# A small copy on GpSimd between the first product of weights and values and the table's transfers

## The chip, the cores and the metric

The kernel runs on one core of a Trainium2 chip. The metric is the device time of one execution in microseconds (us). Before the change the median of three runs is 1701.59 us (1696.14 to 1702.38).

The engines are named as the profile names them: PE is TensorE (PEld its weight loads), DVE is VectorE, ACT is ScalarE, POOL is GpSimd, SP is SyncE, which here only issues transfers. Each engine takes its instructions in order and waits for semaphores of the others.

## The reference

Four layers follow each other on x of 2 batches x 2048 tokens x 256, each added to x: a state-space layer, a mixture of experts, an attention layer and the same mixture of experts again. The change is in the attention layer and in what it shares its time with, the routing of the second mixture.

```python
x = x + attn_a(layernorm(x))            # state space
x = x + ffn(layernorm(x))               # experts, 2 of 8 for each token
x = x + attn_b(layernorm(x))            # attention, below
x = x + ffn(layernorm(x))               # experts, same weights
```

The attention mixes over the first axis of its input, which is the batch, and there are only 2 entries: for each token and each of 16 heads a softmax over two scores. The output is then a weighted sum of two value vectors, projected by w_out and added.

```python
q, k, v = jnp.split(qkv, 3, axis=-1)
scores = jnp.einsum('ibnd,jbnd->ijbn', q, k) * scale
attn = jax.nn.softmax(scores, axis=1)
attn_out = jnp.einsum('ijbn,jbnd->ibnd', attn, v)
return x + attn_out.reshape(slen, bsz, NUM_HEAD * HEAD_DIM) @ w_out.T
```

In an expert layer a router takes the two best of eight experts for each token, and each token's result is the weighted sum of two small networks.

## The kernel before

All products are in float32. Tokens are handled in groups of 512 (four tiles of 128); a group is (b, s), batch b of 2 and stretch s of 4. The attention handles both batches of a stretch together, since it mixes over them; so its loop runs over s = 0 to 3.

**Attention.** A softmax over two scores is a sigmoid of their difference. So the kernel works with xd, the difference of the two normed inputs.
- `scores(s, ts)` (L1328): for each tile of 128 tokens and each half of the heads PE makes pk (keys of xd, PSUM bank A) and two pq (queries of each batch, banks B and C); ACT scales pk into kd (L1351), DVE multiplies (qk, L1355) and sums over the head (L1356).
- `weights(s)` (L1365): ACT's sigmoid, a transpose on PE, a copy to SBUF (prow, L1375), a store to DRAM (prob, L1376), and eight loads on SP (L1382) that repeat each row of prob over 64 partitions: o[0] and o[1], one for each batch, each in four pieces, first those of the value blocks c = 0 to 3, then of 4 to 7. Each of the eight is 512 KB on the SBUF side. Then pv (L1392) adds one batch's own value part.
- `mix(s)` (L1405): for each c of 8 PE makes pvd, the values of xd (L1410, bank A), and DVE multiplies it into o[0] and o[1] in place (L1418).
- `outward(s)` (L1423): for each batch and each pair of tiles PE projects o with w_o (pao, L1430, bank C) and DVE adds to x (L1438). After each batch the routing of its group, `prepared`, is put in line.

Every PSUM bank name (A, B, C, T) has two buffers; PE can be two products ahead of the engine that reads them.

The order of a turn of the loop (L1457): the first half of scores(s + 1), mix(s), outward(s), the second half of scores(s + 1), weights(s + 1). The pieces of other work are generators in `aside`; each call of `aside.step` takes some steps of them: `front` (loads and layer norm of a later stretch), `prepared` and `entered`.

**Routing of the second expert layer.** For each group `prepare` (L309) stores x to the output and the normed xn to DRAM. Its layer norm (L234) has one small step on POOL: rs_g (L244), the power -0.5 of the variance, between DVE's statistics (L239, L240, L243) and DVE's xn_g (L248). PE transposes xn_g (pt_g, L257) and makes the router's scores (pr_g, L330); DVE ranks them and works out a slot in a table in DRAM for every token (L345 to L410). `enter` (L413) then writes the table by indirect transfers from POOL: once, ahead of all others, 16 transfers of `rest` (L420), which fill free slots; then for every group 8 transfers of `pay` (L433). The L433 wait for all L420. Each of these moves 128 rows of 12 bytes. After groups 4 and 6 `plan_early` picks tiles of experts that are already full; SP loads their table rows (tab_ge, L656) and weights (w_ge, L668 and L670), POOL gathers their tokens (xs_ge, L683), PE works on them within the attention stage (L722, L752), and POOL scatters the results (L776).

**What sets the order.** A scheduler orders the traced instructions of each engine but SP, whose order is that of the program. `pool(i)` notes the last instruction of POOL given to it, and the table's transfers are traced in a block that puts them behind that instruction on POOL:

```python
on_pool = []
def pool(i):
    on_pool[:] = [i.ins]
...
with tc.issue_after(on_pool[0]):
    i = nc.gpsimd.indirect_dma_start(out=self.table, ...)
```

Before the change the instruction noted last, where the table's transfers of the attention stage are traced, is a step of a layer norm: rs_l (L1289) or rs_g (L244).

`entered` for the two groups of stretch s is put in line just ahead of mix(s + 1), and mix takes its steps after every second c.

Of the kernel before, what the change touches and what calls it, by code (L numbers as in the profile page):

```python
# [8 lines left out]
F32 = mybir.dt.float32  # L9
# [4 lines left out]
P = 128  # L14
# [32 lines left out]
def kernel(  # L47
# [24 lines left out]
    nc = tc.nc  # L72
# [7 lines left out]
    lnp = ctx.enter_context(tc.tile_pool(name="ln", bufs=2))  # L80
    ps = ctx.enter_context(tc.tile_pool(name="ps", bufs=2, space=bass.MemoryType.PSUM))

    def bank(tag, name):
        return ps.tile([P, 512], F32, tag=tag, name=name)
# [145 lines left out]
    def pool(i):  # L230
        on_pool[:] = [i.ins]
# [994 lines left out]
    with tc.tile_pool(name="att1", bufs=1) as a1, tc.tile_pool(name="att2", bufs=2) as a2:  # L1226
# [178 lines left out]
        def mix(s):  # L1405
            xd, o = inputs.pop(s)[1], mixing[s]
            for c in range(NA):
                pvd = bank("A", f"pvd_{s}{c}")
                for k in range(KD):
                    nc.tensor.matmul(  # L1410
                        pvd,
                        w_qkv_sb[:, k, 2, c * P : (c + 1) * P],
                        xd[:, k, :],
                        start=(k == 0),
                        stop=(k == KD - 1),
                    )
                for i in range(2):
                    nc.vector.tensor_tensor(o[i][:, c, :], pvd, o[i][:, c, :], ALU.mult)  # L1418
                if c % 2:
                    aside.step(2)  # L1420
            mixed.add(s)
# [35 lines left out]
        for s in range(NS):  # L1457

            if s + 1 < NS:
                while s + 1 not in inputs:  # L1460
                    aside.step()
                scores(s + 1, range(0, GT // 2))

                aside.waiting.insert(0, entered())
            else:
                aside.rest()
                tiles.step(4)
            mix(s)
            outward(s)
            if s + 1 < NS:  # L1470
                scores(s + 1, range(GT // 2, GT))
                weights(s + 1)
# [68 lines left out]
```

## Time and profile before

| | |
|---|---|
| median of three runs | 1701.59 us (1696.14 to 1702.38) |
| the profiled execution | 1703.7 us, of which the span from its first to its last instruction is 1702.0 |
| mean granted TensorE clock | 0.97 |
| busy: PE, DVE, ACT, POOL | 1585.8, 896.3, 674.6, 739.0 us |
| PE busy in 0 to 700 us, 700 to 940, 940 to 1400, 1400 to 1702 | 627.7, 227.6, 440.7, 289.8 us |
| transfers by SP's queue, by POOL's queue | 193.42 MB, 36.42 MB |

The four stretches of the third last row are, about: the state-space layer with part of the first expert layer, the rest of that layer, the attention, the rest of the second expert layer.

Lines of the timelines give start, length, engine, line of the kernel, operation, output<-inputs, shapes, the number of merged instructions, and in brackets the idle time before the first of them and what ended it. Buffer numbers are left out of names: o is o[0] or o[1] of any stretch. A transfer's line on POOL or SP is its issue; how long the data took is in the DMA view, "us to landing". "q0 software_dynamic" there is the queue of POOL's transfers, "q1" that of SP's.

### The profile page before, as it was taken

Reading aid. Unit: us, or ns where it says so; the run is one execution under the profiler, and the core shown is the slowest. Engines: PE = TensorE matmul, PEld = TensorE weight load, DVE = VectorE, ACT = ScalarE, POOL = GpSimd, SP = SyncE. Lnnn points to the kernel's source line nnn. Section 1 sums busy time; section 2 is a strip of 40 time slices with the busy share of each in tenths; the row PEclk is TensorE's granted clock in tenths of the full one; section 3 lists DMA queues with packets and bytes.
Section 4 is the critical chain, followed back from the end, with each engine's and each line's share of the span. In section 5 each row is a group of like instructions: output and inputs, shape, how many; then the busy total and the mean of one; then the engine's idle time right before and its main releaser. Section 6 shows DMA issues by size and latency. Waiting matters only on the chain.

```text
span 1702.0 us, 22149 instructions
## 1 busy us (share of the span) xinstructions
PE 1585.8 (93%) x7088; PEld 1194.0 (70%) x7088; DVE 896.3 (53%) x2471; ACT 674.6 (40%) x1340; POOL 739.0 (43%) x702
## 2 busy tenths in 40 slices
PE   6997988989999989999998999899999979999997
PEld 3665555677767767788984575465768768888886
DVE  6778878837648464422227648447454512222222
ACT  5886867856647543222332202011120322333332
POOL 3356457455545556634441003414140751544443
PEclk9998988999989999999999999999999989999999
DMA  4122211743525455889852312516353686888783
GB/s 157 39 63 49 87 47 41 215 125 89 157 48 176 104 148 134 204 261 315 233 112 78 82 43 62 89 50 138 106 107 104 184 226 179 224 236 225 229 215 51
DMA packets 174744, 231.30 MB, mean 136 GB/s; under 512 B 45920, under 2 KB 138080, under 8 KB 174368
## 3 DMA queue, kind: packets, MB, share of 16 engines
q1 hardware_dynamic: 143520, 193.42, 38.7%
q0 software_dynamic: 31104, 36.42, 11.9%
q8 instruction: 58, 0.95, 0.2%
q14 instruction: 62, 0.51, 0.1%
HBM read 192.72 MB, written 37.06 MB: 135 GB/s over the span
## 4 chain that ended last, share of the span: by engine, by line
PE 46%; DMA 7%; DVE 1%; issue 1%; POOL 1%; SPq 0%; ACT 0%; DVEq 0%; POOLq 0%
PE pab_g L722 9%; PE pao L1430 7%; PE pq L1336 6%; PE pab_f L722 5%; PE pf_g L752 4%; PE pvd L1410 3%; PE pab_ge L722 3%; PE pk L1336 3%; DMA out_dram<-y_g,tab_g 2%; PE pf_f L752 2%; DMA o<-prob 2%; PE pf_ge L752 1%; PE pr_g L330 1%; DMA xs_f<-xnd_f,tab_f 1%; DMA resid<-y_f,tab_f 1%
## 5 line engine op out<-in xcount | busy, mean ns | idle before, releaser
L722 PE MATMUL pab_g<-xT_g,w_g 128*128 128x256 f32 (+1 forms) x896 | 181.4, 361 | 0.0
L722 PE MATMUL pab_fe<-xT_fe,w_fe 128*128 128x256 f32 x672 | 158.3, 390 | 20.7 <-DVE gT_fe L731 17.8
L722 PEld LDWEIGHTS pab_g<-xT_g,w_g 128*128 128x128 f32 x896 | 158.4, 190 | 19.6 <-ACT xT_g L713 0.4
L722 PEld LDWEIGHTS pab_fe<-xT_fe,w_fe 128*128 128x128 f32 x672 | 128.8, 195 | 47.7 <-DVE gT_fe L731 22.3
L776 POOL DMA_INDIRECT out_dram<-y_g,tab_g x51 | 80.3, 1575 | 137.0 <-DVE y_g L765 54.9
L730 ACT ACTIVATE sa_g<-pab_g,b_g 128x256 f32<-128x256 f32 (+1 forms) x112 | 51.0, 455 | 188.0 <-PE pab_g L722 188.0
L731 DVE SCALAR_TENSOR_TENSOR gT_g<-pab_g,b_g,sa_g 128x256 f32<-128x256 f32 (+1 forms) x112 | 51.5, 460 | 128.9 <-ACT sa_g L730 128.9
L1336 PE MATMUL pq<-w_qkv_sb,axT 128*128 128x512 f32 x256 | 117.4, 597 | 0.0
L1006 DVE SCALAR_TENSOR_TENSOR xc<-pre,conv_w_sb,xc 128x512 f32<-128x512 f32 x144 | 113.5, 798 | 5.2 <-ACT xc L998 4.6
L1430 PE MATMUL pao<-w_o_sb,o 128*128 128x256 f32 x512 | 112.3, 380 | 0.0
L1430 PEld LDWEIGHTS pao<-w_o_sb,o 128*128 128x128 f32 x512 | 97.0, 190 | 15.9 <-issue 2.9
L989 PE MATMUL pc<-xT,w_in_sb 128*128 128x512 f32 x192 | 96.3, 631 | 0.4 <-ACT xc L998 0.4
L722 PE MATMUL pab_f<-xT_f,w_f 128*128 128x256 f32 (+1 forms) x512 | 96.4, 346 | 0.0
L433 POOL DMA_INDIRECT table_g<-pay_g,at_g x64 | 62.3, 974 | 71.2 <-DVE w_g L409 39.2
L752 PE MATMUL pf_g<-w_g,gT_g 128*128 128x256 f32 x408 | 92.7, 379 | 0.0
L722 PEld LDWEIGHTS pab_f<-xT_f,w_f 128*128 128x128 f32 x512 | 85.5, 191 | 9.4
L1043 ACT ACTIVATE lt<-lb,cum 128x128 f32<-128x128 f32 x256 | 82.8, 394 | 19.8 <-DMA lb<-sums 19.8
L1336 PEld LDWEIGHTS pq<-w_qkv_sb,axT 128*128 128x128 f32 x256 | 48.4, 191 | 57.9 <-issue 56.2
L776 POOL DMA_INDIRECT resid<-y_fe,tab_fe x42 | 67.0, 1595 | 38.2 <-DVE y_fe L765 22.6
L731 DVE SCALAR_TENSOR_TENSOR gT_fe<-pab_fe,b_fe,sa_fe 128x256 f32<-128x256 f32 x84 | 39.7, 480 | 81.3 <-ACT sa_fe L730 81.2
L1351 ACT ACTIVATE kd<-pk 128x512 f32<-128x512 f32 x32 | 19.1, 597 | 159.1 <-PE pk L1336 90.7
L752 PEld LDWEIGHTS pf_g<-w_g,gT_g 128*128 128x128 f32 x408 | 75.4, 190 | 9.3 <-DVE gT_g L731 0.2
(477 smaller groups left out, 3381.9 us busy)
## 6 DMA issues: line engine op xcount, KB each, us to landing
w_g<-in_wl_dram SPq DMA_DIRECT2D x28, 1024.0 KB, 7.5
w_fe<-in_wl_dram SPq DMA_DIRECT2D x21, 1024.0 KB
lb<-sums SPq DMA_DIRECT2D x32, 512.0 KB, 5.8
w_f<-in_wl_dram SPq DMA_DIRECT2D x16, 1024.0 KB, 6.5
o<-prob SPq DMA_DIRECT2D x32, 512.0 KB, 15.6
w_g<-in_wl_dram SPq DMA_DIRECT2D x28, 512.0 KB, 4.0
w_fe<-in_wl_dram SPq DMA_DIRECT2D x21, 512.0 KB, 6.7
w_ge<-in_wl_dram SPq DMA_DIRECT2D x9, 1024.0 KB, 8.4
```

The lines of the kernel that those rows point to most:

```text
L433: i = nc.gpsimd.indirect_dma_start(out=self.table, out_offset=bass.IndirectOffsetOnAxis(ap=at[:, t, c : c + 1], axis=0), in_=pay[:, t, c, ...
L722: nc.tensor.matmul(p[:, q * n : (q + 1) * n], t["w1"][:, k, c * P : (c + 1) * P], t["xT"][:, k, :], start=(k == 0), stop=(k == KD - 1),)
L730: nc.scalar.activation(sa[:, :n], p[:, 0:n], AF.Silu, bias=t["b1"][:, i : i + 1])
L731: nc.vector.scalar_tensor_tensor(t["gT"][:, i, :n], p[:, n : 2 * n], t["b1"][:, NHT + i : NHT + i + 1], sa[:, :n], ALU.add, ALU.mult)
L752: nc.tensor.matmul(pos[h][:, h * DM : (h + 1) * DM], t["gT"][:, j, h * P : (h + 1) * P], t["w2"][:, j, :], start=(j == 0), stop=(j == NHT ...
L776: j = nc.gpsimd.indirect_dma_start(out=self.acc if self.direct else self.acc[: self.seq[i][4] or NT + TT, :], out_offset=bass.IndirectOffs ...
L989: nc.tensor.matmul(pc, w_in_sb[:, k, DI + c * P : DI + (c + 1) * P], xT[:, k, :], start=(k == 0), stop=(k == KD - 1),)
L1006: nc.vector.scalar_tensor_tensor(xc[:, c, :], pre[:, c, j : j + TG], conv_w_sb[:, c, j : j + 1], xc[:, c, :], ALU.mult, ALU.add,)
L1043: nc.scalar.activation(lt[:, i, :], lb[:, i, :], AF.Relu, bias=g["cum"][:, t, i : i + 1], scale=-1.0)
L1336: nc.tensor.matmul(p, src[:, k, t * P : (t + 1) * P], w_qkv_sb[:, k, j, half * TG : (half + 1) * TG], start=(k == 0), stop=(k == KD - 1),)
L1410: nc.tensor.matmul(pvd, w_qkv_sb[:, k, 2, c * P : (c + 1) * P], xd[:, k, :], start=(k == 0), stop=(k == KD - 1),)
L1430: nc.tensor.matmul(po[:, j * DM : (j + 1) * DM], o[i][:, c, (t + j) * P : (t + j + 1) * P], w_o_sb[:, c, :], start=(c == 0), stop=(c == NA ...
```

## The change

In `mix`, after the products of the first value block, POOL copies one column of o[1] into a tile of its own, which nothing reads; `pool` notes the copy. There are four such copies in the kernel, one for each stretch.

```diff
                 for i in range(2):
                     nc.vector.tensor_tensor(o[i][:, c, :], pvd, o[i][:, c, :], ALU.mult)
+                if c == 0:
+
+                    come = lnp.tile([P, 1], F32, tag="come", name=f"come{s}")
+                    pool(nc.gpsimd.tensor_copy(come, o[1][:, c, 0:1]))
                 if c % 2:
                     aside.step(2)
```

In the order that the scheduler makes of it, the instructions of PE, DVE, ACT and SP stand as before. On POOL the copy of s = 0 stands ahead of the first rs_g; that of s = 1 ahead of the 16 transfers of L420 and the 16 of L433 that follow them; that of s = 2 ahead of the next 16 of L433; that of s = 3 behind the 16 transfers of L433 of stretch 2 and some gathers and scatters, ahead of the next rs_g. After the copy of s = 1 POOL's order is: 16 of L420, 16 of L433, rs_g twice, the copy of s = 2, 16 of L433, four gathers (L683), rs_g twice.

## The prediction

> **What bounds the kernel now.** I read the page first: TensorE (PE) is busy 93% of the span and holds 46% of the chain that ended last, so a change of order elsewhere counts only where PE waits. The diff touches the attention stage (about 940 to 1400 us), so next came the chain and the timelines of that stage.
>
> The chain of waits around the second mix (s = 1), columns start, length, what:
>
> ```profile
> 1059.41 0.91 PE pt_m L257 x8
> ...
> 1060.42 23.41 DMA o<-prob
> ...
> 1083.85 0.70 DVE o L1418
> ```
>
> The timeline of PE over the same mix:
>
> ```profile
> 1074.74 3.60 PE L1410 MATMUL pvd<-axd,w_qkv_sb 128*128 128x512 f32 x8
> 1084.60 12.04 PE L1410 MATMUL pvd<-axd,w_qkv_sb 128*128 128x512 f32 x24 [6.26 <-DVE o L1418]
> 1096.47 27.79 PE L1430 MATMUL pao<-w_o_sb,o 128*128 128x256 f32 x128
> 1124.10 1.88 PE L1336 MATMUL pk<-w_qkv_sb,axd 128*128 128x512 f32 x4
> 1125.81 3.60 PE L1336 MATMUL pq<-w_qkv_sb,axT 128*128 128x512 f32 x8
> ```
>
> PE starts the mix at 1074.74, fills both buffers of bank A, and sits until DVE can multiply o[1], which waits for a transfer of probabilities issued at 1060.42. The first mix has no such hole: its 32 matmuls take 13.80 us (980.39 to 994.19 in the chain). Here 1074.74 to 1096.47 is 21.73. **The hole is worth 21.73 - 13.80 = 7.9 us.**
>
> Why is that transfer slow? The DMA view of the first mix's transfers (955 to 1000 us), then of the second's (1050 to 1090); the GB/s row has 40 equal slices:
>
> ```profile
> GB/s 0 0 0 0 42 16 25 275 206 226 200 226 204 211 211 206 220 204 218 195 228 200 226 193 67 9 0 0 0 0 0 0 0 0 0 0 0 0 0 0
> ...
> o<-prob SPq DMA_DIRECT2D x8, 512.0 KB, 8.6
> ```
>
> ```profile
> GB/s 0 0 0 2 2 67 1 1 2 28 39 0 219 193 39 55 90 80 137 253 181 158 172 97 27 23 33 181 268 184 100 160 182 244 207 229 229 187 143 55
> ...
> q0 software_dynamic: 512, 0.03, 1.4%
> ...
> o<-prob SPq DMA_DIRECT2D x8, 512.0 KB, 23.4
> table_g<-rest_g,free POOLq DMA_INDIRECT x16, 13.4
> ```
>
> Alone, the 4 MB run at a flat 200 GB/s or so. Beside the table's transfers they fall below 60 several times. Those transfers start where GpSimd (POOL) is free, right after the last rs_l; POOL's timeline:
>
> ```profile
> 1049.69 1.63 POOL L1289 TENSOR_TENSOR rs_l<-rs_l,mhalf 128x8 f32<-128x8 f32 x1 [5.30 <-DVE rs_l L1288]
> 1051.49 1.06 POOL L420 DMA_INDIRECT table_g<-rest_g,free  x1 [0.17 <-issue]
> ...
> 1068.12 0.96 POOL L420 DMA_INDIRECT table_g<-rest_g,free  x1 [0.31 <-issue]
> 1077.66 0.96 POOL L420 DMA_INDIRECT table_g<-rest_g,free  x1 [8.58 <-DMA table_g<-rest_g,free]
> ...
> 1090.00 0.96 POOL L433 DMA_INDIRECT table_g<-pay_g,at_g  x1 [10.12 <-DMA table_g<-rest_g,free]
> ...
> 1109.80 0.95 POOL L433 DMA_INDIRECT table_g<-pay_g,at_g  x1 [0.30 <-issue]
> 1112.53 1.04 POOL L244 TENSOR_TENSOR rs_g<-rs_g,mhalf 128x4 f32<-128x4 f32 x1 [1.78 <-DVE rs_g L243]
> ```
>
> The last two lines matter most: the 32 transfers end at 1110.75, and rs_g, which DVE asks for at 1112.4, stands behind them on POOL with 1.78 us to spare.
>
> **The change, part by part.** In the changed program the order on PE, DVE, ACT and SP is what it was; POOL's differs by four copies alone. Copies 0 and 3 stand in POOL's idle time (69.39 us before 1010.02, 28.15 us before 1298.76) and hold up nothing: 0. Copy 1 stands ahead of the 32 transfers of s = 1, copy 2 ahead of 16 of s = 2, and each waits for o[1]'s first product of its mix. No copy of 128x1 is in the trace; the nearest are a copy of 128x18 at 0.20 us (L985) and another at 0.85 (L1016), and a memset of 128x1 at 0.10. It is an added instruction, so no gain; I take 0.2, ends 0.1 and 0.85.
>
> *Gain in mix 1.* With the transfers held back, o[0] is multiplied at 1076.80 as before and o[1] directly after, done at 1076.80 + 1.29 = 1078.09. That needs its transfer landed by 1077.5, 17 us after the issue at 1060.42. In s = 3, beside weight loads, the same product could start 16.2 us after the first of its issues (1253.98 to 1270.20); in s = 0 all eight were through 22 us after theirs, and the first four go first. PE then runs through: -7.9 us. Ends: -6.3 (only the hole itself) and -7.9.
>
> Here a rule of the Trainium skill speaks against the gain. DMA: Bandwidth & Descriptors, section SWDGE vs HWDGE vs iDMA, has the software queue and SP's queue in separate internal queues of each DMA engine, served in turn by packets. By that the table's packets should delay the others only by their own time, 1.4% of the 40 us window or 0.6 us, and holding them back would gain 0.6. This trace doesn't agree: 23.4 us to landing against 8.6 for the same transfers of s = 0. By the rule the sum below would be +6 and not -0.3. I take the rows, and keep the rule's case as a rival, since s = 2 kept some 210 GB/s beside 16 table transfers (landing 17.4).
>
> *Cost at rs_g of s = 1.* The transfers now start late, and rs_g is still behind them. POOL wakes 0.15 after DVE (1112.38 to 1112.53), copy 0.2, next start 0.17: first L420 at 1078.6. Sixteen at 1.28 start to start (16.63 / 13): the last at 1097.8. L433 waits for it to land: 3.0 to 4.4 for the four issued before o<-prob, 5.8 for the median L433 after 1090, 6.9 the longest; I take 4.4, then 0.8 from landing to start (1078.92 + 10.3 to 1090.00): 1103.0. Sixteen L433 take 20.75 (1090.00 to 1110.75): 1123.8. So POOL is taken for 45.2 us against 59.3 before, but 27 us later. rs_g starts at 1124.1, DVE's xn_g 1.08 later (1112.53 to 1113.61), its four take 1.38, and the queued x<-pao 0.69: done at 1127.2.
>
> Behind that wait on DVE stand x<-pao of the second batch, its statistics and all qk of the next scores; they free the buffers of bank C. PE goes on through both remaining pao, pk and the first pq, and stops at the second pq, which needs the C buffer that x<-pao frees. Before, that pq began at 1125.81 + 1.72 = 1127.53, thus 1119.6 with 7.9 taken off. **PE waits 1127.2 - 1119.6 = 7.6 us.** By the ends of landing: 6.2 (3.0), 9.0 (5.8), 10.1 (6.9); the copy adds up to 0.65. The next stop, the fifth pq, needs the buffer that qk's first product frees: DVE is done with it near 1133.7, PE gets there near 1135.8, so no second hole.
>
> *Cost in s = 2.* No gain: PE went into that mix at 1175.58 without a wait. The 16 L433 move from 1152.71 to 1178.92 + 0.5 = 1179.4, the last is issued at 1199.2 and lands near 1205 (5.8). Behind it on SP are the first two tab_ge (8 us behind the last L433 before), the weights of two tiles, three more tab_ge and the stores of s = 2: all some 20 us later, and first used by PE at 1247.4: hidden. On POOL four gathers wait for tab_ge, 2.75 after its issue: 1207.8 to 1212.5, and rs_g moves from 1205.44 to 1212.8. DVE's xn_g is done at 1215.3, and PE's pt_g that reads it stood at 1217.00: **hidden by 1.7 us**; past that, each us costs one.
>
> *Sum.* -7.9 + 7.6 + 0 = -0.3 us. On the profiled 1703.7 (span 1702.0 and 1.7 outside it) that is 1703.4. That run was 2.1 above the median 1701.59, so I predict 1701.3.
>
> **Rivals.**
> 1. *The table is not what slows o<-prob* (the rule above, and s = 2). Copy 1 then ends near 1084.9 and the same 45.2 us end at 1130; x<-pao at 1133.7 against pq at 1127.5: +6, or 1707.6. Against it: s = 0 has no table transfer and no dip.
> 2. *Slower: the block on POOL stays long.* If the moved transfers land as slowly as before (POOL taken for 59.3 us), rs_g starts 14.1 later still and PE waits 21.7: 7.9 is won, +13.8 in all, 1715.4. It passes 0.5% (8.5 us) where the block exceeds 45.2 + 8.8 = 54 us. For it: waits of 8.58 and 10.12 stand in the trace. Against: both fell beside o<-prob, which is over by about 1080.
> 3. *The gain without the price:* -7.9, 1693.7. The block would have to end by 1116.2, 37.6 us after its start, while 31 steps of 1.28 alone are 39.7. Only a partial form is left, with the smallest landing: -1.7.
> 4. *The bind does nothing,* because the transfers are not moved: the program's order on POOL excludes it.
>
> **How the numbers follow.** The sum with its ends (1699 to 1706): 0.58. Rival 1 (1706 to 1709): 0.14. Rival 2 (1709 to 1716), with a hole in s = 2 as its small form: 0.20. Rival 3 and gains I do not see (1692 to 1698): 0.08. The range 1695 to 1712 leaves out the far half of rivals 2 and 3. About 0.5% (8.5 us) is what a measurement of this kernel can tell from no change: faster by more 0.06, within 0.76, slower by more 0.18.
>
> **What would show it.** PE's pvd of s = 1 in one piece of about 14 us with no wait for DVE's o; o<-prob landing in 9 to 13 us with a flat GB/s row; the first L420 about 3 us after PE's second mix starts; DVE's xn_g waiting near 21 us for POOL's rs_g once (1104.5 to 1125.1), where its longest wait is 1.5 now; PE waiting 6 to 9 us at a pq after the second pao. I am wrong if xn_g does not wait (then faster), or if L420 or L433 wait for landings of over 8 us again (then slower), or if pt_g of s = 2 waits for xn_g.

## The result, and the profile after

The changed kernel takes 1704.2 us (median of 22 runs, 1697.5 to 1710.9) against 1697.8 of before on the same chip (22 runs, 1686.7 to 1707.1): a ratio of 1.0029, 95% interval 1.0015 to 1.0043, or 4.9 us slower (1697.8 x 0.0029). I had forecast 0.3 us faster: the sign and the sum were wrong.

The second mix went as forecast. I call the 16 transfers of L420 the fill, the 16 of L433 the token transfers, and all that the copy of s = 1 now holds back on POOL, up to rs_g, the block. The timeline of PE after (columns: start, length, engine, line, operation, tiles, shapes, count, idle time before and what ended it; lines from L1422 on stand four higher than before):

```profile
1070.69 13.96 PE L1410 MATMUL pvd<-axd,w_qkv_sb 128*128 128x512 f32 x32
1084.49 27.79 PE L1434 MATMUL pao<-w_o_sb,o 128*128 128x256 f32 x128
1112.11 1.88 PE L1336 MATMUL pk<-w_qkv_sb,axd 128*128 128x512 f32 x4
1113.83 1.88 PE L1336 MATMUL pq<-w_qkv_sb,axT 128*128 128x512 f32 x4
1128.40 3.78 PE L1336 MATMUL pq<-w_qkv_sb,axT 128*128 128x512 f32 x4 [12.69 <-DVE x L1442]
1131.97 3.07 PE L1336 MATMUL pk<-w_qkv_sb,axd 128*128 128x512 f32 x4
```

From pvd to pao it is 13.80 us where before took 21.73: the hole of 7.9 is gone. The DMA view of 1050 to 1090 us shows why: from 1054 to 1072 us, while o<-prob runs, the rate is flat, and the first table transfer is issued at 1074.44.

```profile
GB/s 0 66 0 109 276 199 229 197 215 211 197 229 197 219 211 197 229 199 219 211 193 233 195 31 0 0 2 2 18 1 1 2 2 2 1 1 2 0 1 2
```

But at the second pq PE waits 12.69 us and not the forecast 7.6, and the four pq behind the hole take 3.78 us instead of 1.88, the next four pk 3.07. The timeline of POOL after has the reason for the first of these:

```profile
1074.09 0.19 POOL L1422 COPY come<-o 128x1 f32<-128x1 f32 x1 [26.82 <-DVE o L1418]
1074.44 1.08 POOL L420 DMA_INDIRECT table_g<-rest_g,free  x1 [0.16 <-issue]
...
1094.02 0.95 POOL L420 DMA_INDIRECT table_g<-rest_g,free  x1 [0.30 <-issue]
1104.86 0.96 POOL L433 DMA_INDIRECT table_g<-pay_g,at_g  x1 [9.89 <-DMA table_g<-rest_g,free]
...
1124.31 0.95 POOL L433 DMA_INDIRECT table_g<-pay_g,at_g  x1 [0.30 <-issue]
1125.28 1.05 POOL L244 TENSOR_TENSOR rs_g<-rs_g,mhalf 128x4 f32<-128x4 f32 x1
```

The copy costs 0.19. Between the last fill (L420) and the first token transfer (L433) POOL waits 9.89 us for the landing, with o<-prob long over. The block from 1074.44 to 1125.28 is 50.8 us where I had 45.2, and rs_g starts as soon as it ends. The waits of the attention stage (engine, tile, line, releaser: sum, count, longest):

```profile
DVE xn_g L248 <- POOL rs_g L244: 37.7, 8, 26.0
...
PE pq L1336 <- DVE x L1442: 12.7, 1, 12.7
```

The second reason is PE's clock. A table by stretches has the granted clock behind the five engines' busy times (1.00 is full), then the DMA share and GB/s. After:

```profile
1070.70:1084.50 13.80, 13.80 (x34) 5.94 (x33) 10.83 (x16) 0.00 (x0) 8.01 (x9) 1.00 0.21 39
1084.50:1112.00 27.50, 27.50 (x129) 24.22 (x128) 5.98 (x15) 0.00 (x0) 13.25 (x14) 1.00 0.08 21
1112.00:1140.00 28.00, 15.31 (x30) 6.42 (x29) 10.60 (x25) 1.20 (x2) 12.27 (x13) 0.76 0.17 57
...
1128.40:1132.00 3.60, 3.60 (x5) 1.53 (x6) 2.66 (x10) 0.00 (x0) 0.72 (x1) 0.50 0.72 257
...
1134.90:1140.00 5.10, 5.10 (x13) 2.27 (x12) 3.36 (x4) 0.60 (x1) 0.00 (x0) 1.00 0.24 85
```

The clock is at half when PE comes back, and full again from 1134.90 on. The same table of before gives 0.84 for its mix with the hole (0.56 for 1084.60 to 1088.00, right behind it), and 1.00 after it. So the new hole costs 12.7 and 3.1 more ((3.78 - 1.88) + (3.07 - 1.88)), and the measure that I use from here on, the start of the second mix to the start of the third, goes from 100.8 us (1074.74 to 1175.58) to 108.8 (1070.69 to 1179.50): -7.9 and +15.9.

This pair of profiles shows +8.0 where the medians show 4.9 (2.5 to 7.3). Nothing in step s = 2 took the difference back: from the third mix to the fourth it is 72.8 us in both. The two executions can't be compared as wholes: after's ended 4.3 us earlier (1697.7 against 1702.0), because its first mix began 4.1 us earlier and all that follows the last pao took 378.6 us against 388.8 (from the fourth mix to the last pao it was 2.0 longer). The same changed kernel took 393.2 there in e10 below, so this is no gain of the change that I could claim.

In s = 2 the change was hidden, as forecast: the copy starts at 1182.91, rs_g at 1212.93, and PE waits for nothing at pt_g.

### The profile page after: what moved, and what is told of

The parts are those of the page before. It is cut to its first block, busy times and chain, and to the rows that moved or that the text cites. A ratio compares the mean times of both kernels' runs of the same rounds, so it can differ in the third digit from the quotient of the medians.

```text
span 1697.7 us, 22159 instructions
## 1 busy us (share of the span) xinstructions
PE 1583.7 (93%) x7088; PEld 1192.0 (70%) x7088; DVE 894.6 (53%) x2471; ACT 674.7 (40%) x1340; POOL 737.0 (43%) x706
## 4 chain that ended last, share of the span: by engine, by line
PE 47%; DMA 5%; POOL 3%; DVE 1%; issue 1%; ACT 0%; SPq 0%; DVEq 0%; POOLq 0%
PE pab_g L722 9%; PE pq L1336 6%; PE pab_f L722 5%; PE pao L1434 5%; PE pf_g L752 4%; PE pk L1336 3%; PE pab_ge L722 3%; PE pf_f L752 3%; PE pvd L1410 2%; DMA out_dram<-y_g,tab_g 2%; PE pf_ge L752 1%; POOL table_g L433 1%; POOL table_g L420 1%; PE pr_g L330 1%; DMA xs_f<-xnd_f,tab_f 1%
## 5 line engine op out<-in xcount | busy, mean ns | idle before, releaser
L1336 PE MATMUL pq<-w_qkv_sb,axT 128*128 128x512 f32 x256 | 120.3, 609 | 12.7 <-DVE x L1442 12.7
L1434 PEld LDWEIGHTS pao<-w_o_sb,o 128*128 128x128 f32 x512 | 97.0, 190 | 15.9 <-issue 2.9
L752 PE MATMUL pf_fe<-w_fe,gT_fe 128*128 128x256 f32 x336 | 79.3, 389 | 2.2 <-DVE gT_fe L731 2.2
```

What stands on the lines that cost most here:

```text
L752: nc.tensor.matmul(pos[h][:, h * DM : (h + 1) * DM], t["gT"][:, j, h * P : (h + 1) * P], t["w2"][:, j, :], start=(j == 0), stop=(j == NHT ...
L1336: nc.tensor.matmul(p, src[:, k, t * P : (t + 1) * P], w_qkv_sb[:, k, j, half * TG : (half + 1) * TG], start=(k == 0), stop=(k == KD - 1),)
L1434: nc.tensor.matmul(po[:, j * DM : (j + 1) * DM], o[i][:, c, (t + j) * P : (t + j + 1) * P], w_o_sb[:, c, :], start=(c == 0), stop=(c == NA ...
```

## The experiments

My theory: the copy of s = 1 (copy 1) closes the hole in the mix and pays for it at rs_g, with a price set by the length of POOL's block: issues, landing, issues. Rivals: copy 2 (of s = 2) carries the loss; or any table transfer, not only this order, does harm wherever it lies. Twelve runs follow; "stretch" is the start of the second mix to that of the third, from PE's timeline. All but e8 are timed beside before on the same chip, where before has medians of 1721 to 1725 us.

| run | what is different | stretch, us | ratio to before | 95% interval |
|---|---|---|---|---|
| before (first chip) | | 100.8 | | |
| after (first chip) | four copies | 108.8 | 1.0029 | 1.0015 to 1.0043 |
| e1 | copy of s = 1 alone | 107.3 | 1.0033 | 1.0018 to 1.0048 |
| e2 | copy of s = 2 alone | 103.7 | 1.0011 | 0.9996 to 1.0026 |
| e3 | L433 of two groups behind rs_g | 102.1 | 1.0004 | 0.9988 to 1.0021 |
| e4 | before, no fill | 100.3 | 0.9985 | 0.9967 to 1.0002 |
| e5 | after, no fill | 92.9 | 0.9946 | 0.9925 to 0.9967 |
| e6 | after, fill to another table | 112.7 | 1.0069 | 1.0046 to 1.0092 |
| e7 | fill and L433 behind rs_g | 119.4 | 1.0106 | 1.0077 to 1.0136 |
| e8 | e3 once more | 103.1 | a single run | |
| e9 | e3, paced | 102.2 | 0.9994 | 0.9983 to 1.0006 |
| e10 | after itself | 106.8 | 1.0008 | 0.9993 to 1.0023 |
| e11 | e9, four buffers of at_g | 92.9 | 0.9940 | 0.9919 to 0.9960 |
| e12 | e3, four buffers of at_g | 101.7 | 0.9994 | 0.9978 to 1.0010 |

The stretch accounts for the times: with e2, whose second mix has before's order, as the base (103.7 us), a difference of the stretches over 1723 us gives e5 and e11 -0.63%, e6 +0.52%, e7 +0.91%, e1 +0.21%, e10 +0.18%, all within the measured intervals. Before was not profiled on these chips; with its 100.8 of the first chip as the base, e10 (+0.35%) falls outside.

**Which copy.** e1 keeps the copy of s = 1 alone, e2 that of s = 2 alone:

```diff
-                if c == 0:
+                if c == 0 and s == 1:
```

> Only the copy of s = 1 is kept. Theory (all of the price is the block of 32 table transfers that copy 1 moves ahead of rs_g of s = 1): as the whole change, about +5 us or 1.003; PE's second mix in one piece of 13.8, then a wait of PE near 12.7 us at the second pq behind x<-pao, DVE's xn_g waiting 26 us for rs_g once. Rival (the price comes from copy 2, which makes table rows, weights and gathers of the early tiles later): copy 1 alone is at 0 to -3 us, and PE's stretch from the third to the fourth mix is shorter than with the whole change.

> Only the copy of s = 2 is kept. Theory: nothing, 1.000 within 0.2%: the hole in the second mix stays at about 6.3 us (o<-prob landing near 23), the gathers and rs_g of s = 2 come 4 to 8 us later than before and no PE instruction waits for them. Rival (price in s = 2 or in the early tiles): +2 to +5 us, with PE waiting at pt_g of s = 2 or longer from the start of mix 3 to its end (37.2 before, 39.2 with the whole change).

Measured: e1 slower by 0.33%, with the mix in one piece and PE's wait of 11.2 us at the pq; e2 keeps the hole (6.0 us) and shows no clear difference. Copy 1 carries gain and price; for copy 2 neither shows.

**The price apart from the gain.** e3 leaves the fill behind the copy and puts the token transfers of both groups behind the two rs_g of s = 1; the order on the other four engines stays:

```diff
-                aside.waiting.insert(0, entered())
+                aside.waiting.insert(0, filled() if s == 1 else entered())
...
+            if s == 1:
+                aside.add(token_rows())
```

> All four copies kept; of the 32 transfers behind copy 1 the 16 of L433 are traced later, behind both rs_g of s = 1; the order on PE, DVE, ACT and SP is that of the change. Theory: the gain stays (mix 2 in 13.8 us) and the price goes, since 16 fill transfers end 20.5 us after the copy, ahead of DVE's request for rs_g: -7 to -8 us against before, 0.995 to 0.996; DVE's xn_g waits at most 2 us for rs_g, PE has no wait at the pq after the second pao. Rival (the price is the copies, or the table being later at all): +3 to +8 us against before, since here the table's rows of the first groups come later still.

Measured: no clear difference (1.0004), not the theory's 0.995. The mix is whole and PE doesn't wait at the pq, so the price at rs_g is gone; but DVE and ACT wait at sc_g and kd, and then PE. DVE's line, and PE's, of e3:

```profile
1151.01 0.19 DVE L338 TENSOR_TENSOR sc_g<-pr_g,br_sb 128x32 f32<-128x32 f32 x1 [8.77 <-remote]
```

```profile
1153.95 0.60 PE L363 MATMUL pk_g<-sel_g,tri 128*128 128x32 f32 x2 [6.30 <-DVE sel_g L357]
```

"Remote" means that the profile finds no work that ended when the signal came. PE's pr_g are over at 1144.12, so DVE got their signal 6.9 us late; by the records of signals, three of PE's came together at 1150.99 to 1151.09, just behind the last of 16 token transfers (issued 1147.34). So a new wait took the place of the old one. It comes back below; first the other side, the gain.

**Does the fill alone slow o<-prob?** e4 is before without the 16 transfers of L420; the filling of free slots is left out.

> The kernel before without the 16 fill transfers (L420): free slots of the table keep their first contents, so that part of the computation is left out. The 16 of L433 then start right behind rs_l, at the place of the fill. Theory (it is the fill transfers that slow o<-prob, at about 2 us each to land, where L433 beside o<-prob in s = 2 left its rate alone): the hole in the second mix goes, -7 to -8 us, 0.995. Rival (any table transfer beside o<-prob slows it): the hole stays at 4 us or more, -1 to -4 us.

Measured: 0.9985, no clear difference; the rival's case. The token transfers then start beside o<-prob, and the mix still has two small holes (1.93 and 2.22 us). Its DMA view from 1060 to 1105 us dips to 51 even without the fill:

```profile
GB/s 0 0 0 0 1 0 58 3 1 1 1 1 40 18 44 15 25 36 261 254 206 214 216 194 70 51 73 130 236 228 204 224 217 229 208 186 124 53 0 0
```

So both kinds of table transfer can cost beside o<-prob. The rule weighed in the prediction (the Trainium skill, DMA: Bandwidth & Descriptors, section SWDGE vs HWDGE vs iDMA: queues served in turn, so 0.6 us by the prediction's estimate) does not hold for these rows, since holding the transfers back gave 7.9. It is not refuted everywhere: in s = 2 of before, 16 token transfers run beside the same eight loads and the rate stays flat (1150 to 1184 us):

```profile
GB/s 0 0 0 0 0 79 2 19 2 2 32 7 116 195 227 261 212 195 228 224 198 221 212 214 210 224 200 216 210 216 211 195 197 238 180 102 25 0 0 0
```

What makes the difference between s = 1 and s = 2 was not tried.

**The block's length.** e5 is after without L420 (the filling is left out): a block of 16 issues and no landing to wait for.

> The changed kernel without the 16 transfers that fill the free slots (L420); the filling is left out, so that the copy is followed on GpSimd by the 16 token transfers alone. My theory (the price is the length of GpSimd's block between the copy and rs_g: 16 issues of 1.28 us, 10.1 us of landing, 16 issues more): the block falls from 50.8 to about 21 us, rs_g no longer waits for it (it is wanted about 28 us after the copy), PE has no hole at the pq after the second mix, its clock doesn't drop there, and the second mix stays in one piece (13.4 us): 7.9 us less than before, a ratio of 0.995. Rival (the price comes from the copy's wait itself or from the binding, whatever is behind it): still 10 us or more of waiting at that pq, a ratio near 1.003.

Measured: 0.9946, as the theory has it. POOL of e5:

```profile
1088.75 0.19 POOL L1413 COPY come<-o 128x1 f32<-128x1 f32 x1 [26.82 <-DVE o L1409]
1089.10 1.08 POOL L424 DMA_INDIRECT table_g<-pay_g,at_g  x1 [0.16 <-issue]
...
1108.68 0.96 POOL L424 DMA_INDIRECT table_g<-pay_g,at_g  x1 [0.30 <-issue]
1115.21 1.04 POOL L244 TENSOR_TENSOR rs_g<-rs_g,mhalf 128x4 f32<-128x4 f32 x1 [5.57 <-DVE rs_g L243]
```

rs_g now waits for its own input and not for POOL. The copy, the order behind it and the move to a later time are the same as in after; only the block is 20.5 us long and not 50.8. The rival that the copy's wait, or binding transfers to it, costs as such is out.

e6 was to take the landing alone out of the block: the fill goes to a table that nobody reads (the free slots are not filled), and L433 waits for nothing.

```diff
-                                out=self.table,
+                                out=self.aside,
...
-                        self.freed.append(i.ins)
```

> The changed kernel with the 16 fill transfers written to a table of their own that nobody reads (so the free slots are not filled), and the token transfers without their wait for them: 32 issues and no landing between. Theory: the block is 50.8 less 9.1 of waiting, 41.7 us; PE's hole at the pq falls from 12.7 to about 3.6 us; if the clock is not halved after so short a hole the sum is 7.9 less 3.6, 4.3 us less than before, a ratio of 0.9975; if it is, about 0.999. Rival (the landing is not the term that was mis-sized, the issues behind it are slowed as much): the hole stays near 12 us, a ratio of 1.003.

Both expectations failed: 1.0069. The issues did close up to 41 us (1098.17 to 1138.91), but PE itself slowed down in the middle of it. PE of e6:

```profile
1108.22 14.50 PE L1434 MATMUL pao<-w_o_sb,o 128*128 128x256 f32 x66
...
1127.06 0.58 PE L1434 MATMUL pao<-w_o_sb,o 128*128 128x256 f32 x1 [1.02 <-issue]
1129.16 1.28 PE L1434 MATMUL pao<-w_o_sb,o 128*128 128x256 f32 x2 [1.52 <-issue]
1132.66 0.58 PE L1434 MATMUL pao<-w_o_sb,o 128*128 128x256 f32 x1 [2.22 <-issue]
...
1142.46 13.35 PE L1434 MATMUL pao<-w_o_sb,o 128*128 128x256 f32 x51 [0.82 <-issue]
```

and DVE's second x<-pao waited 22.27 us, "remote" too, some 21 us past the end of its matmuls. From 1122.7 to 1142.4 PE did 6.0 us of work, waiting for nothing that the profile names, and was at full work again 3.5 us after the last of the 32 (1138.91). It may be that the pause of 9 us for the landing, which I wanted out of the block, had kept the transfers from piling up; no run shows that. Because of PE's stall, e6 says nothing on the size of the landing term.

**A better place for the block?** e7 puts all 32 behind the two rs_g. Its edit, against e3:

```diff
-            yield from last.fill()
-            for _ in range(8):
+            for _ in range(16):
                 yield
```

> The fill and the token transfers of the second and third group both behind the two rs_g of the second step, everything else in the order of the changed kernel on every engine. Theory: the second mix in one piece (7.9 us less than before), no price at rs_g, and a block of GpSimd of 51 us from about 15 us before the third product chain, over before the copy of the third step: a ratio of 0.995. Rival (as in the run that moved only the token transfers: a signal of PE reaches VectorE and ScalarE some 6 us late near the end of a series of transfers, wherever it lies, and PE waits for it): a ratio of 1.000.

> The kernel of e3_split once more, for its trace alone. If the 8.8 us that VectorE and ScalarE waited at sc_g and kd there belong to this order of the work, they come again at the same place; if they are an accident of that execution, the stretch from the end of the second mix to the third is near 79.5 us instead of 88.8.

Measured: e7 1.0106, the slowest of all; the rival's late signal is there (sc_g waits 8.5 us), and a second wait, which I hadn't foreseen. e8 shows e3's stall again at the same place (8.62 us), so it belongs to this order and not to one execution. The new wait of e7:

```profile
1171.70 0.16 DVE L391 TENSOR_TENSOR at_g<-lo_g,hi_g 128x4 int32<-128x4 f32 x1 [14.44 <-DMA table_g<-pay_g,at_g]
```

The row numbers at_g have two buffers, and a token transfer reads them from SBUF: moved late, it holds up the group after next, and PE stands 13.49 us behind that.

**Pace, and buffers.** e9 is e3 with a pow of 128x4 behind each pair of these transfers, and 4 of the 16 fills with the token transfers. e11 has four buffers for at_g as well, e12 the buffers without the pace. Nothing is left out in any of them. Of the edits, the pause and the buffers:

```diff
+            with tc.issue_after(behind.ins):
+                pool(nc.gpsimd.tensor_tensor(z, ones[:, :GT], mhalf, ALU.pow))
...
-            at = rt2.tile([P, GT, 2], I32, tag="at", name=f"at_{nm}")
+            at = rt2.tile([P, GT, 2], I32, tag="at", name=f"at_{nm}", bufs=4)
```

> As e3_split, nothing left out, but with a pow of 128x4 of about 1.05 us on GpSimd behind each pair of the fill's and of these token transfers, so that they are issued some 1.9 us apart instead of 1.28; 12 of the 16 fill transfers behind the copy, 4 with the token transfers behind the two rs_g. Theory (a rate, not a latency: transfers into the table land about 1.8 us apart, and what is issued faster waits in a queue): issued at 1.9 us the landing no longer grows from 4 towards 10 us but stays at 3 to 5 us for all. If the late signals of PE (x, sc_g) come of the same queue, they come on time, the stretch from the second mix to the third is near 79.5 us again and the ratio is 0.995. Rival: the landing grows all the same (the slots' addresses, not the pace), or PE's signals are late whatever the pace; then the ratio is 1.000 or above.

> The changed kernel itself on this chip, beside the run with the paced transfers: second mix in one piece (13.4 us), xn_g waiting over 20 us for rs_g, a hole of 11 to 13 us of PE at the pq behind it and a halved clock of PE after the hole; a ratio of 1.003.

> As e9_paced, with four buffers instead of two for the tile at_g (the row numbers that a token transfer reads from SBUF). In e9_paced VectorE waited 4.6 us at at_g for the transfers of two groups before, and PE 4.1 us for VectorE at pr_g, at half clock for a while after. Theory (with pacing no signal of PE is late, and with the buffers nobody waits for a transfer to have been read): the stretch from the end of the second mix to the third falls from 88.8 to near 79.5 us and the ratio to 0.995. Rival (another wait takes its place again): 88 us, 0.999.

> As e3_split, not paced, with four buffers for at_g. If the signals of PE that came 6 to 7 us late at sc_g need a series of 16 transfers at 1.28 us, they come again here and the stretch stays near 88 us, a ratio of 1.000; if the buffer was what held that run too, the stretch is near 79.5 us and the ratio 0.995, as with pacing.

Measured: e9 0.9994. The late signals at sc_g are gone, but DVE waits 4.64 us at at_g, PE waits 4.05 us behind it and then runs at a granted clock of 0.50 for a while (pr_g x14 take 3.00 us where they take 1.62 in e11). By the signals of the transfers themselves the fill's landing still grew, to 8.5 us at the eighth, and fell to 4.6 at the twelfth, where after's eighth took 9.7 and its last 10.1: with the pace it is lower, but not the 3 to 5 that I expected. e12 0.9994, with sc_g waiting 8.7 us again. PE of e9, then DVE of e12:

```profile
1161.63 0.60 PE L331 MATMUL pr_g<-wr_sb,rxT_g 128*128 128x8 f32 x2 [4.05 <-DVE prow L1407]
```

```profile
1157.86 0.19 DVE L338 TENSOR_TENSOR sc_g<-pr_g,br_sb 128x32 f32<-128x32 f32 x1 [8.68 <-remote]
```

e11, with both, has 0.9940 (0.9919 to 0.9960): the stretch is 92.9 us, all of the forecast gain with no price (100.8 less 7.9), and the timeline shows no wait of PE in it. PE of e11:

```profile
1099.59 2.31 PE L1442 MATMUL pvd<-axd,w_qkv_sb 128*128 128x512 f32 x5
1101.74 27.79 PE L1466 MATMUL pao<-w_o_sb,o 128*128 128x256 f32 x128
1129.37 1.88 PE L1368 MATMUL pk<-w_qkv_sb,axd 128*128 128x512 f32 x4
1131.08 3.60 PE L1368 MATMUL pq<-w_qkv_sb,axT 128*128 128x512 f32 x8
...
1151.77 0.30 PE L364 MATMUL pk_g<-sel_g,tri 128*128 128x32 f32 x2
```

POOL of e11, where rs_g waits for its input and the transfers stand apart:

```profile
1111.42 0.97 POOL L421 DMA_INDIRECT table_g<-rest_g,free  x1 [0.30 <-issue]
1112.41 1.05 POOL L437 TENSOR_TENSOR pause_g<-ones,mhalf 128x4 f32<-128x4 f32 x1
1117.73 1.01 POOL L245 TENSOR_TENSOR rs_g<-rs_g,mhalf 128x4 f32<-128x4 f32 x1 [4.28 <-DVE rs_g L244]
```

e11 is 0.6% faster than before; against the changed kernel it was not timed directly. e10, the changed kernel beside e9, gives 1.0008 and no clear difference, where 1.003 was expected: its hole is nearly the same (12.1 us), but only the pq behind it are slow (3.51; the pk take 1.88), and before's mix seems to be longer there (e2's, with the same order, 22.2 us from the first pvd to the last against 21.3, and 2.0 us more behind it). So the changed kernel's loss is 0.3% on the first chip and not clear from none on e10's; whole mix, wait for rs_g and hole at the pq are the same in all three traces (after, e1, e10).

## Why the prediction was wrong

- **The hole in the mix: right.** -7.9 forecast, 21.73 to 13.80 measured; o<-prob undisturbed; the first L420 3.75 us after the mix starts (3.9 forecast). The trace's rows beat the rule.
- **The copies: right.** 0.19 us (0.2), with 0 in s = 0, 2 and 3.
- **The price at rs_g: right in place and chain, wrong in size. The step that failed is "L433 waits for it to land: ... I take 4.4".** It was 10.1 us from the issue of the last L420 (1094.02) to its landing. The 5.7 missing make the block 50.8 instead of 45.2 us, and PE's wait 12.7 instead of 7.6. With 10.1 in place of 4.4 the sum would have been +5.4. I had read the landing of the sixteenth fill from the first four, as if it were the same for all. In after, too, the first two land in 3.0 us; but counted from the issue to a transfer's last signal, the third takes 9.0, the eighth 9.7, the thirteenth 6.0 and the sixteenth 10.1. The row of the same rank stood in before's timeline: the wait of 10.12 was for the landing of its sixteenth fill, and I set it aside as an effect of o<-prob. In after o<-prob is over and the wait is 9.89. (The 8.58 was something else: the fifteenth fill waiting for an earlier one, whose landing took 17.0 us beside o<-prob.)
- **What sets the landing stays open.** Rank and pace alone do not. The views of after, for the fill, for the token transfers right behind it, and for those of s = 2, all issued about 1.3 us apart (each view knows the landing of 10 of the 16):

```profile
DMA to landing us min/median/max: 2.9/7.5/9.4
...
DMA to landing us min/median/max: 4.3/5.5/7.6
...
DMA to landing us min/median/max: 2.7/3.0/4.5
```

- **A term that was missing: the clock after the hole.** 3.1 us in after, 1.6 in e10. The rows had it: before's hole was a wait of 6.26 us, and cost 7.9. I booked the whole 7.9 as gain and gave the new hole its bare length. In after PE was at half clock for some 6 us behind the hole, in e10 for about half as long (granted clock 0.53 from 1145.60 to 1149.00, then 1.00). The Trainium skill, TensorE: Matmul & The Clock Gate, section The HAM clock gate, says that PE runs at half clock after an idle window of about 3.4 us, until it has been busy for about as long; half of 3.4 us lost is 1.7 as an estimate from that page, near e10's 1.6 and well short of after's 3.1. With both measured terms the sum is +8.5, the trace +8.0.
- **s = 2 hidden: right.** No wait at pt_g.
- **Rival 2** had the sign and half the mechanism: the wait of "over 8 us again" came, but the block's end at 50.8 us lay between my value and its 59.3. I gave it 0.20 with an argument that after refutes: the wait came though o<-prob was over. Rival 1 is out by the mix; rival 3 could not be had by the copy, but e11 shows that the gain without the price exists in another order.

What stays open: why the stretch differs by 8.0 us and the medians by 4.9; what makes the fill land so late; and what it is in a long series of table transfers that holds up PE's signals.

## What to carry to other kernels

When something waits for a series of transfers, take the landing of the last one of that very series from the trace: here 10.1 us where the first took 3.0, and another series at the same pace never took more than 4.5. Book a hole of PE by what its removal gives back, wait and slow clock, and charge a new hole the same way. Moving a block of work to a later time wins only if nobody needs the same engine at that time: look for the next instruction of another owner there (here rs_g), and for the buffers that the late work still reads (here at_g).

## What the runs showed of the hardware

- A transfer of 128 rows of 12 bytes into the table, issued about every 1.3 us, landed after 3.0 us (the first two of the fill in after), after 6.0 to 10.5 (the other 14), or after 2.7 to 4.5 (the token transfers of s = 2 in the same trace). Waits for the last of the 16 fills to land were 6.8 to 10.3 us in five kernels.
- Beside series of 16 such issues without a pause PE's signal to DVE came some 7 us late at sc_g in four traces (e3, e7, e8, e12). The same lateness stands at the first x<-pao of s = 1 in e1, e2, e3, e5, e8, e10 and e12, where DVE waits 7.8 to 12.3 us, marked remote, and 4.42 in after; there it found slack, and PE lost 2.0 us at most (e2). In e6, with 32 in a row, it was some 21 us, and PE's own matmuls stood apart without a named wait. With issues some 1.8 us apart no signal was late, and e11 shows both cases in one execution: none beside its paced series in s = 1, and one beside the 16 that follow the copy of s = 2 (1184.25) at full pace. DVE of e11:

```profile
1207.22 0.69 DVE L1474 TENSOR_TENSOR x<-pao,x 128x512 f32<-128x512 f32 x1 [10.65 <-remote]
```

- By what way the series holds up PE's signals was not tried. before's and after's profiles on the first chip show no late signal beside such series, and e10, the same kernel as after, has two; so it depends on something besides the kernel. For the loss, pace and buffers together removed it, and neither alone.
- o<-prob falls from some 210 GB/s to 20 to 60 where table transfers run beside it in s = 1 of before and e4, though these take 1.4 and 2.5% of the engines' time there; in s = 2 of before it does not fall.
